# A graph network on one core: features normalised in place, the convolutions' buffers in two pools, and the check of the edge order moved into the second convolution

## The chip, the cores and the metric

The kernel runs on one core of a Trainium2 chip. A core has TensorE (PE; its weight loads are shown apart as PEld), VectorE (DVE), ScalarE (ACT), GpSimd (POOL) and SyncE (SP, which here only issues transfers). Each engine works off its own instructions strictly in the order in which the program lists them. The metric is the device time of one execution in microseconds (us); less is better. A run's time is compared as a median over several executions.

## The reference: what is computed

There are 12,500 nodes with 64 features each and 200,000 edges (`src`, `dst`), the list being sorted by `dst`, and 64 features for each edge. In short:

```python
h = relu(layernorm(x))
h1 = relu(mean_over_edges_into(dst, h[src]) @ W1l.T + b1 + h @ W1r.T)
x = x + mean_over_edges_into(dst, h1[src]) @ W2l.T + b2 + h1 @ W2r.T
h = relu(layernorm(x))
hidden = relu(concat(h[src], h[dst], edge_attr) @ W1 + b1)
x = x + mean_over_edges_of(src, hidden @ W2 + b2)
```

All is float32. The kernel keeps each float32 table as three bfloat16 parts that add up to it.

## The kernel before, in words

**Tiling.** Nodes go in 49 blocks of 256. The edges into one block lie in one window of 128 × 34 entries of the sorted list; where a window begins is worked out on the chip. Inside a window the edges are sorted by the block of their `src`, into 49 cells of at most 128 slots. So there are 49 × 49 = 2401 cells, and each cell joins one source block with one destination block.

**A cell in a convolution.** The numbers of a cell's source nodes are a row in DRAM (`srow_b`). SP loads the rows of 16 cells, broadcast to all partitions, as one tile `srow` of 512 KB (L725). DVE compares it with the partition's node number, which gives the one-hot `turned` (L735). PE multiplies it with the three-part table (`ta` in the first convolution, `tb` in the second) into `got` (L889), ACT casts that to `rows` (L893), DVE makes the one-hot of the destinations, `hot` (L744), and PE adds the rows up in `acc` (L769). After the 49 cells of a destination block `conv` closes it (L806 to L843): ACT copies the sums (L816), DVE forms the mean (L820 to L828), PE transposes and multiplies with the weights (L834, L839), and DVE adds the bias (L841). The first convolution writes its result as three parts into `tb`, the second goes on to the layer norm of the last stage.

**The start.** Four pieces of work are woven into each other by hand: every piece is a generator, and a `yield` is a place where the other pieces get their turn.

* `find_blocks` (L19 to L109) loads the whole `dst` list as 125 × 1600 integers (`find_d`), checks that it does not go down (L31 to L42: each entry against the next; the entry at a row's end by a small tile `find_n` that two more transfers fill), shifts the numbers down to block numbers (L47, L50), counts with small matmuls where each block begins, and leaves `begin_i` (L98) and `bad` (L103). At its end the flags of the order check are transposed by PE (L105) and join `bad` (L108, L109).
* `features` (L470 to L497) normalises x, which lies in the memory of `tb`, in seven parts: a layer norm (L322 to L340), then the split into three parts (L342 to L352) with subtractions on POOL. The normalised values go from `ln_sq` through a Relu into a tile `h1`, the rests into `three_r`. These tiles are in a pool `in` with three buffers.
* `sorter` (L509 to L688) sorts the edges of one block after the other in 13 steps on DVE and PE, and writes the rows (`rows_o`) to DRAM by SP's queue (L660 to L662).
* `clearing` (L270 to L287) fills tables in DRAM with zeros, from a part of `tb` that POOL has set to zero (L700), in transfers of 640 KB and 160 KB on SP's queue.

POOL's `seen` (L699) waits for the last load of x before POOL sets that part to zero, and the integer ramps of `find_blocks` (L53, L57) are behind it on POOL.

**The order around the convolutions.** The convolutions run over groups of 4 cells. The transfers of `srow` are issued two parts of 16 cells ahead. While the first convolution runs, the sorter and the clearing go on; in both, `edge_terms` (POOL's indirect transfers, L385) runs beside. At the end of the first convolution a copy of `bad` goes to `which` (L958), which after the last stage selects between this path's result and a general one.

**Pools and memory.** A tile's memory is given out by its pool. The pool `in` takes the top end of what is free, the pool `layers` (`srow`, `turned`, `hot`, `rows`, then the tiles of `conv`) the other end; `layers` is opened after `in` is closed and partly lies on the same memory. An instruction that writes such memory first waits for the last instruction that used it. Transfers that SP and ACT issue take eight completion semaphores in turn, so each waits for the transfer eight before it.

Of the kernel before, what the change touches and what calls it, by code (L numbers as in the profile page):

```python
# [15 lines left out]
P = 128  # L16


def find_blocks(tc, work, psum, begin_i, bad, dst, nb, blk, win):  # L19
# [8 lines left out]
    d = work.tile([R, C], I32, name="find_d")  # L28
    nc.sync.dma_start(d, dst.rearrange("(r c) -> r c", c=C))

    n = work.tile([R, 2], I32, name="find_n")  # L31
    rows = dst.rearrange("(r c) -> r c", c=C)
    nc.vector.memset(n, 0)
    nc.sync.dma_start(n[0:R - 1, 0:1], rows[0:R - 1, C - 1:C])
    nc.sync.dma_start(n[0:R - 1, 1:2], rows[1:R, 0:1])
    yield
    down = work.tile([R, C], BF, name="find_down")
    nc.vector.tensor_tensor(down[:, 0:C - 1], d[:, 0:C - 1], d[:, 1:C], op=OP.is_gt)
    nc.vector.tensor_tensor(down[:, C - 1:C], n[:, 0:1], n[:, 1:2], op=OP.is_gt)
    yield  # L40
    flags = work.tile([R, 1], FT, name="find_flags")
    nc.vector.tensor_reduce(flags, down, AX.X, OP.max)  # L42


    yield
    q = d
    nc.vector.tensor_scalar(q, d, blk.bit_length() - 1, None, op0=OP.arith_shift_right)  # L47
    yield
    qb = down
    nc.vector.tensor_copy(qb, q)  # L50
    yield
    ids_i = work.tile([R, nb], I32, name="find_ids_i")
    nc.gpsimd.iota(ids_i, pattern=[[1, nb]], base=0, channel_multiplier=0)  # L53
# [6 lines left out]
    first = work.tile([R, 1], FT, name="find_first")  # L60
    nc.vector.tensor_copy(first, q[:, 0:1])
# [13 lines left out]
    for k in range(0, C, F):  # L75
        yield
        pr = psum.tile([nb, F], FT, name="find_pr", bufs=2)
        nc.tensor.matmul(pr, pick, qb[:, k:k + F], start=True, stop=True)
# [22 lines left out]
    nc.vector.tensor_sub(many, line[:, 1:], begin)  # L101
    nc.vector.tensor_scalar(many, many, float(win), None, op0=OP.is_gt)
    nc.vector.tensor_reduce(bad, many, AX.X, OP.max)  # L103
    pf = psum.tile([1, P], FT, name="find_pf")
    nc.tensor.transpose(pf[:, :R], flags, ident[:R, :R])  # L105
    yield
    f = work.tile([1, 1], FT, name="find_f")
    nc.vector.tensor_reduce(f, pf[:, :R], AX.X, OP.max)  # L108
    nc.vector.tensor_max(bad, bad, f)  # L109

@with_exitstack
def fast_path(
# [197 lines left out]
    def bc(ap, n):  # L313
        return ap.unsqueeze(len(ap.shape)).to_broadcast([*ap.shape, n])
# [154 lines left out]

    def features():  # L470
        def some(work, s):
            h = work.tile([P, 2 * CH, D], FT, name="h1", bufs=2)
            xs = xs_all[s].rearrange("p b h d -> p (b h) d")
            yield from layernorm_relu(work, h, xs, 2 * CH, xs)
            yield from three(work, ta[:, s * CH:(s + 1) * CH].rearrange("p b h d -> p (b h) d"), h,
                             nc.gpsimd.tensor_sub)

        def others():
            for _ in range(2):
                if next(finding, found) is found:  # L480
                    found[0] = True
            if sorted_to[0] < STEPS:
                next(sorter)
            next(clearing, None)

        with tc.tile_pool(name="in", bufs=3, side="right") as work:
            line = Line()
            for s in range(NB // CH):
                line.tick(some(work, s))
                others()  # L490
                line.tick()
                others()
# [307 lines left out]
    gather = layers.enter_context(tc.tile_pool(name="gather_ps", bufs=4, space=bass.MemoryType.PSUM))  # L800
    work = layers.enter_context(tc.tile_pool(name="layers", bufs=2))
    next_rows = rows_with_one(work)
    line = Line()
    second = [None]

    def conv(layer, table, w, b, finish, B, acc):  # L806

        if layer:
            xv = second[0].tile([P, 2, D], FT, name="x2", bufs=3)
            if B == FULL:  # L810
                nc.vector.memset(xv[96:P], 0.0)
            a, t = node_rows(x, B, xv)
            nc.sync.dma_start(t, a)
        yield
        v = work.tile([P, 2, W3], FT, name="sums")
        nc.scalar.copy(v, acc[:, :, :W3])  # L816
        yield
        m = work.tile([P, 2, 2, D], FT, name="both")
        t = table[:, B]
        nc.vector.tensor_add(m[:, :, 1], t[:, :, 0:D], t[:, :, D:2 * D])  # L820
        nc.vector.tensor_add(m[:, :, 1], m[:, :, 1], t[:, :, 2 * D:])
        nc.vector.tensor_add(m[:, :, 0], v[:, :, 0:D], v[:, :, D:2 * D])
        nc.vector.tensor_add(m[:, :, 0], m[:, :, 0], v[:, :, 2 * D:D3])
        if layer == 0:
            c = work.tile([P, 2], FT, name="cnt")
# [9 lines left out]
        ct = work.tile([P, 2, P], FT, name="both_t")  # L835
# [4 lines left out]
        o = work.tile([P, 2, D], FT, name="conv")  # L840
        nc.vector.tensor_add(o, acc[:, :, P:P + D], rows(b, 2))  # L841
        yield
        yield from finish(B, o, *((xv,) if layer else ()))  # L843

    def after_conv1(B, o):
        g = work.tile([P, 2, D], FT, name="g", bufs=3)
        nc.scalar.activation(g, o, AF.Relu)
        yield from three(work, tb[:, B], g, nc.vector.tensor_sub)

    def after_conv2(B, o, v):  # L850
        nc.vector.tensor_add(v, v, o)
# [88 lines left out]
    for (layer, c0, c1, part), t, coming in ahead(  # L940
            todo, lambda p: sources(*p[:3]),
            lambda p, r: turned(work, "turned", r, p[2] - p[1])):
        for a, z in part:
            line.tick_behind(some_cells(layer, t, c0, a, z))
            if layer == 0:
                sort_to(z)
                while filled < z:
                    filled += next(clearing, CELLS)
            next(coming, None)
            if layer or a >= 150:  # L950
                beside.passed((z - a) * (1.1, 0.9)[layer])
# [475 lines left out]
```

## Time and profile before

Three runs took 3668.18, 3670.29 and 3679.0 us; the median is 3670.29. The profile shows another execution:

| what | value |
|---|---|
| time of the profiled execution | 3675.2 us |
| its span, first to last instruction | 3673.4 us |
| mean granted TensorE clock | 0.989 of full |
| the start, until the first `turned` | 0 to 90.15 us |
| first convolution | to about 1307 us |
| copy of `bad` to `which` (L958) | 1307.49 us |
| load of `find_d` (781 KB) issued | 0.76 us |

How it is read: a line of the timeline gives the start in us, the length in us, the engine, the program's line, the operation, the tile written and the tiles read with partitions × elements and type, and `xN` where several lie together. In brackets stand the idle time of the engine ahead of it and what ended that. "SPq" is an issue of a transfer on SP's queue, not the transfer itself. "issue" as releaser means that the profile shows nothing that was waited for. A row of windows gives for each stretch its length, then the busy time and the number of instructions of PE, PEld, DVE, ACT and POOL, the granted clock, the mean busy share of the 16 DMA engines, and GB/s.

### The profile page before, as it was taken

To read this page: it belongs to the slowest core of one execution; us is meant where nothing else is said; L and a number is where in the kernel's file an instruction comes from. 1 tells how busy PE (TensorE), PEld (TensorE's weight loads), DVE (VectorE), ACT (ScalarE), POOL (GpSimd) and SP (SyncE) were. 2 spreads that over 40 slices of the span, in tenths; PEclk is the share of its full clock that TensorE was granted. 3 is DMA by queue.
4 is the path that set the end of the run, shared out by engine and by line. 5 is a ranking of instruction groups with operands and counts; after the bars stand their busy time and mean duration, and the time that the engine had idled before them with its cause. 6 is when DMAs were issued, how large, how long until landed. Compare 5 with 4: busy or idle time off the path is not lost.

```text
span 3673.4 us, 126991 instructions
## 1 busy us (share of the span) xinstructions
PE 3419.6 (93%) x50925; PEld 3363.3 (92%) x50925; DVE 3253.3 (89%) x5709; ACT 2506.4 (68%) x5944; POOL 2756.2 (75%) x2335
## 2 busy tenths in 40 slices
PE   1799999899899999999999998999999999999897
PEld 0798999898889999999999998999999999999887
DVE  7999999999899868778787787899989998998998
ACT  3455656565566667777777776788888888887665
POOL 4067787888777877777777773788888888887665
PEclk9999999999999999999999999999999999999999
DMA  6755545555454334444444444766666676666664
GB/s 212 269 163 152 169 155 162 156 167 160 142 164 143 122 120 146 129 141 140 137 137 137 141 129 142 225 215 200 220 208 216 202 219 210 210 201 206 191 219 145
DMA packets 413671, 635.66 MB, mean 173 GB/s; under 512 B 94131, under 2 KB 296247, under 8 KB 413070
## 3 DMA queue, kind: packets, MB, share of 16 engines
q1 hardware_dynamic: 353106, 572.87, 49.9%
q0 software_dynamic: 53312, 51.36, 4.1%
q8 instruction: 399, 6.54, 0.7%
q10 hardware_dynamic: 6652, 3.24, 0.4%
q14 instruction: 202, 1.65, 0.1%
HBM read 474.72 MB, written 155.83 MB: 172 GB/s over the span
## 4 chain that ended last, share of the span: by engine, by line
PE 64%; DVE 24%; DMA 5%; issue 3%; POOL 2%; SPq 1%; ACT 1%; ACTq 0%; DVEq 0%; POOLq 0%
PE acc L769 23%; PE got L889 13%; PE got L1071 12%; PE got L1072 6%; DVE hot L744 6%; DVE turned L735 4%; PE pE L417 3%; DVE hot_r L629 3%; PE pE L402 2%; POOL terms L385 2%; DMA terms_in<-terms 1%; DVE ranks L617 1%; DMA terms<-tb 1%; PE got L1068 1%; PE acc L839 1%
## 5 line engine op out<-in xcount | busy, mean ns | idle before, releaser
L385 POOL DMA_INDIRECT terms<-terms_o,turn_i x1666 | 1929.8, 1158 | 625.9 <-issue 425.1
L893 ACT CAST rows<-got 128x384 bf16<-128x384 f32 x2402 | 1038.3, 485 | 666.0 <-PE got L889 655.2
L769 PEld LDWEIGHTS <-hot 128*128 128x128 bf16 x12006 | 1032.2, 99 | 14.4 <-issue 4.8
L769 PE MATMUL acc<-rows,hot 128*128 128x193 bf16 x9604 | 1010.6, 247 | 0.0
L1083 POOL TENSOR_TENSOR hidden<-hidden 128x512 f32<-128x512 f32 (+1 forms) x602 | 758.5, 1260 | 227.7 <-ACT hidden L1080 144.0
L889 PEld LDWEIGHTS <-turned 128*128 128x128 bf16 x9604 | 813.3, 98 | 89.6 <-DVE turned L735 60.4
L744 DVE TENSOR_TENSOR hot<-dcol,local 128x1024 bf16<-128x1024 bf16 x1202 | 807.9, 683 | 12.7 <-PE acc L769 11.6
L735 DVE TENSOR_SCALAR turned<-srow,nid 128x2048 bf16<-128x2048 bf16 (+1 forms) x906 | 779.4, 874 | 22.7 <-issue 10.8
L1071 PE MATMUL got<-ta,turned 128*128 128x128 bf16 x3920 | 599.1, 220 | 7.3 <-DVE turned L735 7.3
L1071 PE MATMUL got<-tb,turned_d 128*128 128x128 bf16 x3920 | 599.8, 220 | 1.1 <-DVE turned_d L735 1.1
L889 PE MATMUL got<-ta,turned 128*128 128x192 bf16 x4802 | 508.4, 248 | 73.3 <-DVE turned L735 49.4
L1072 PE MATMUL got<-tb,turned_d 128*128 128x64 bf16 x3920 | 546.0, 193 | 0.0
L1072 PE MATMUL got<-ta,turned 128*128 128x64 bf16 x3920 | 545.9, 193 | 0.0
L1095 ACT ACTIVATE hot_a<-every,scol 128x256 bf16<-128x256 bf16 x1196 | 505.4, 493 | 0.0
L889 PE MATMUL got<-tb,turned 128*128 128x192 bf16 x4802 | 494.1, 246 | 0.9 <-DVE turned L735 0.5
L1080 ACT ACTIVATE hidden<-y 128x512 f32<-128x512 f32 (+1 forms) x301 | 190.4, 633 | 270.4 <-DVE y L1077 154.8
L1071 PEld LDWEIGHTS <-turned 128*128 128x128 bf16 x3920 | 362.4, 98 | 8.2 <-issue 7.8
L1071 PEld LDWEIGHTS <-turned_d 128*128 128x128 bf16 x3920 | 359.7, 98 | 1.7 <-DVE turned_d L735 1.7
L1072 PEld LDWEIGHTS <-turned 128*128 128x128 bf16 x3920 | 359.2, 98 | 1.2
L1072 PEld LDWEIGHTS <-turned_d 128*128 128x128 bf16 x3920 | 359.6, 98 | 0.0
L1098 ACT ACTIVATE hot_a<-hot_a 128x1024 bf16<-128x1024 bf16 x299 | 316.2, 1057 | 9.5
L735 DVE TENSOR_SCALAR turned_d<-drow,nid 128x2048 bf16<-128x2048 bf16 (+2 forms) x302 | 316.8, 1091 | 0.0
(220 smaller groups left out, 4912.2 us busy)
## 6 DMA issues: line engine op xcount, KB each, us to landing
srow<-srow_b SPq DMA_DIRECT2D x300, 512.0 KB
srow<-srow_k SPq DMA_DIRECT2D x149, 512.0 KB
drow<-drow_k SPq DMA_DIRECT2D x149, 512.0 KB
terms_in<-terms SPq DMA_DIRECT2D x294, 160.0 KB
edges<-in_edge_attr_dram SPq DMA_DIRECT2D x200, 192.0 KB
terms<-tb SPq DMA_DIRECT2D x200, 160.0 KB
terms<-tb SPq DMA_DIRECT2D x48, 640.0 KB
terms<-terms_o,turn_i POOLq DMA_INDIRECT x1666
```

What stands on the lines that cost most here:

```text
L385: nc.gpsimd.indirect_dma_start(out=terms[j][:], out_offset=bass.IndirectOffsetOnAxis(ap=at[:, c, h:h + 1], axis=0), in_=o[:, c, h], in_off ...
L735: nc.vector.tensor_scalar(o[:, h, :n * S], r[:, :n * S], nid[:, h:h + 1], None, op0=OP.is_equal)
L744: nc.vector.tensor_tensor(o[:, :n], cols.rearrange("p (g c) -> p g c", c=2).unsqueeze(2).to_broadcast([P, n, 2 * P, 2]), local.rearrange(" ...
L769: nc.tensor.matmul(self.acc[B][:, h, :W3], lt, r[:, c, 0:W3], start=k + h == 0, stop=k == row - 1 and h == 1, skip_group_check=True)
L889: nc.tensor.matmul(p[:, (i - c) * D3:(i - c + 1) * D3], t[:, h, (a - c0 + i) * S:(a - c0 + i + 1) * S], table[:, (a + i) % NB, h], start=h ...
L893: nc.scalar.copy(g[:, c:c + m, :D3], p[:, :m * D3].rearrange("p (c d) -> p c d", c=m))
L1071: nc.tensor.matmul(p[:, c], lt, rt[:, 0:2 * D], start=i == 0, stop=False, skip_group_check=True)
L1072: nc.tensor.matmul(p[:, c, 0:D], lt, rt[:, 2 * D:], start=False, stop=i == 3, skip_group_check=True)
L1080: nc.scalar.activation(w[:, :n, 0:D], y[:, :n], AF.Relu)
L1083: nc.gpsimd.tensor_sub(w[:, :n, (i + 1) * D:(i + 2) * D], w[:, :n, j], upper(w)[:, :n, j])
L1095: nc.scalar.activation(q[:, c - k], every, AF.Abs, scale=-1.0, bias=scol[:, scol_at[last] + a + c:scol_at[last] + a + c + 1])
L1098: nc.scalar.activation(q[:, :n - k], q[:, :n - k], AF.Relu, bias=1.0, scale=-2.0)
```

## The change

1. `find_blocks` no longer checks the order. `find_n`, its two transfers, `find_down`, `find_flags`, the transpose and the last two DVE instructions are gone, and with them two yields. The shift and its cast come first; the cast goes to an own tile `find_q`, and `find_first` is copied right behind it.
2. `features` works in place: the normalised values and the rests stay in the memory of `tb`, `h1` and `three_r` are gone, and the pool `in` has two buffers for three. Numbers and kinds of the instructions stay.
3. The tiles of `conv` and `after_conv1` (`sums`, `both`, `cnt`, `both_t`, `conv`, `g`, `three_r`) leave the pool `layers` for a pool `closing`, opened after it. In memory `in` now begins above the part of `layers` that holds `srow`, `turned`, `hot` and `rows`.
4. `order_check` is new. It is opened at the end of the first convolution and goes one step on with every group of the second: it loads the whole `dst` list again, with a 1601st column that holds the first entry of the next row, compares in two halves, takes maxima in halves and quarters, reduces, lets PE transpose, and joins the result with `bad`. Only then is `bad` copied to `which`.

As a consequence, the program's order moves a little elsewhere: DVE's L554 and L555 of the next blocks' sorting come ahead of the first `turned`.

```diff
@@ find_blocks
-    n = work.tile([R, 2], I32, name="find_n")
-    rows = dst.rearrange("(r c) -> r c", c=C)
-    nc.vector.memset(n, 0)
-    nc.sync.dma_start(n[0:R - 1, 0:1], rows[0:R - 1, C - 1:C])
-    nc.sync.dma_start(n[0:R - 1, 1:2], rows[1:R, 0:1])
     yield
-    down = work.tile([R, C], BF, name="find_down")
-    nc.vector.tensor_tensor(down[:, 0:C - 1], d[:, 0:C - 1], d[:, 1:C], op=OP.is_gt)
-    nc.vector.tensor_tensor(down[:, C - 1:C], n[:, 0:1], n[:, 1:2], op=OP.is_gt)
+    nc.vector.tensor_scalar(d, d, blk.bit_length() - 1, None, op0=OP.arith_shift_right)
     yield
-    flags = work.tile([R, 1], FT, name="find_flags")
-    nc.vector.tensor_reduce(flags, down, AX.X, OP.max)
-    yield
-    q = d
-    nc.vector.tensor_scalar(q, d, blk.bit_length() - 1, None, op0=OP.arith_shift_right)
-    yield
-    qb = down
-    nc.vector.tensor_copy(qb, q)
+    q = work.tile([R, C], BF, name="find_q")
+    nc.vector.tensor_copy(q, d)
+    first = work.tile([R, 1], FT, name="find_first")
+    nc.vector.tensor_copy(first, d[:, 0:1])
     yield
...
-    pf = psum.tile([1, P], FT, name="find_pf")
-    nc.tensor.transpose(pf[:, :R], flags, ident[:R, :R])
+
+
+def order_check(tc, work, psum, ident, bad, dst):
...
+    rows = dst.rearrange("(r c) -> r c", c=C)
+    d = work.tile([R, C + 1], I32, name="order_d")
+    nc.vector.memset(d[96:R, C:], 2 ** 30)
+    nc.sync.dma_start(d[:, 0:C], rows)
+    nc.sync.dma_start(d[0:R - 1, C:], rows[1:R, 0:1])
+    for _ in range(4):
+        yield
+    down = work.tile([R, C], BF, name="order_down")
+    nc.vector.tensor_tensor(down[:, 0:C // 2], d[:, 0:C // 2], d[:, 1:C // 2 + 1], op=OP.is_gt)
     yield
-    f = work.tile([1, 1], FT, name="find_f")
-    nc.vector.tensor_reduce(f, pf[:, :R], AX.X, OP.max)
+    nc.vector.tensor_tensor(down[:, C // 2:], d[:, C // 2:C], d[:, C // 2 + 1:], op=OP.is_gt)
+    yield
+    for k in (C // 2, C // 4):
+        nc.vector.tensor_max(down[:, 0:k], down[:, 0:k], down[:, k:2 * k])
+    yield
+    flags = work.tile([R, 1], FT, name="order_flags")
+    nc.vector.tensor_reduce(flags, down[:, 0:C // 4], AX.X, OP.max)
+    yield
+    p = psum.tile([P, 512], FT, name="pX")
+    nc.tensor.transpose(p[0:1, :R], flags, ident[:R, :R])
+    yield
+    f = work.tile([1, 1], FT, name="order_f")
+    nc.vector.tensor_reduce(f, p[0:1, :R], AX.X, OP.max)
     nc.vector.tensor_max(bad, bad, f)
@@ features
-            h = work.tile([P, 2 * CH, D], FT, name="h1", bufs=2)
-            xs = xs_all[s].rearrange("p b h d -> p (b h) d")
-            yield from layernorm_relu(work, h, xs, 2 * CH, xs)
-            yield from three(work, ta[:, s * CH:(s + 1) * CH].rearrange("p b h d -> p (b h) d"), h,
-                             nc.gpsimd.tensor_sub)
+            n = 2 * CH
+            v = xs_all[s].rearrange("p b h d -> p (b h) d")
+            o = ta[:, s * CH:(s + 1) * CH].rearrange("p b h d -> p (b h) d")
...
+            nc.vector.reciprocal(st[:, 1], st[:, 2])
+            nc.vector.tensor_mul(v, v, bc(st[:, 1], D))
+            yield
+            nc.scalar.activation(v, v, AF.Relu)
+            nc.scalar.copy(o[:, :, 0:D], v)
+            yield
+            nc.gpsimd.tensor_sub(v, v, o[:, :, 0:D])
+            yield
+            nc.scalar.copy(o[:, :, D:2 * D], v)
+            yield
+            nc.gpsimd.tensor_sub(o[:, :, 2 * D:], v, o[:, :, D:2 * D])
...
-        with tc.tile_pool(name="in", bufs=3, side="right") as work:
+        with tc.tile_pool(name="in", bufs=2, side="right") as work:
@@ the convolutions
+    closing_work = layers.enter_context(tc.tile_pool(name="closing", bufs=2))
...
-        v = work.tile([P, 2, W3], FT, name="sums")
+        v = closing_work.tile([P, 2, W3], FT, name="sums")
...
             if layer:
+                if ordered is not None and next(ordered, ordered) is ordered:
+                    ordered = None
+                    ordering.close()
+                    nc.vector.tensor_copy(which, bad)
...
-            nc.vector.tensor_copy(which, bad)
             sorting.close()
+            ordering = ExitStack()
+            ordered = order_check(tc, ordering.enter_context(tc.tile_pool(name="order", bufs=1, side="right")),
+                                  psum_x, ident, bad, dst)
```

More of the change, by code (lines that the diff above doesn't have):

```diff
@@ L59, in find_blocks @@
     nc.vector.tensor_copy(own, own_i)
-    first = work.tile([R, 1], FT, name="find_first")
-    nc.vector.tensor_copy(first, q[:, 0:1])
     less = work.tile([R, nb], FT, name="find_less")
@@ L77, in find_blocks @@
         pr = psum.tile([nb, F], FT, name="find_pr", bufs=2)
-        nc.tensor.matmul(pr, pick, qb[:, k:k + F], start=True, stop=True)
+        nc.tensor.matmul(pr, pick, q[:, k:k + F], start=True, stop=True)
         nc.vector.tensor_scalar(row[:, k:k + F], pr, own[:nb], None, op0=OP.is_lt)
@@ L103, in find_blocks @@
     nc.vector.tensor_reduce(bad, many, AX.X, OP.max)
-    pf = psum.tile([1, P], FT, name="find_pf")
-    nc.tensor.transpose(pf[:, :R], flags, ident[:R, :R])
-    yield
-    f = work.tile([1, 1], FT, name="find_f")
-    nc.vector.tensor_reduce(f, pf[:, :R], AX.X, OP.max)
+def order_check(tc, work, psum, ident, bad, dst):
+    nc = tc.nc
+    R = 125
+    C = dst.shape[0] // R
+    rows = dst.rearrange("(r c) -> r c", c=C)
[7 more added lines that the diff above has]
+    nc.vector.tensor_tensor(down[:, 0:C // 2], d[:, 0:C // 2], d[:, 1:C // 2 + 1], op=OP.is_gt)
+    yield
+    nc.vector.tensor_tensor(down[:, C // 2:], d[:, C // 2:C], d[:, C // 2 + 1:], op=OP.is_gt)
[11 more added lines that the diff above has]
+    nc.vector.tensor_reduce(f, p[0:1, :R], AX.X, OP.max)
     nc.vector.tensor_max(bad, bad, f)
@@ L471, in some @@
         def some(work, s):
-            h = work.tile([P, 2 * CH, D], FT, name="h1", bufs=2)
-            xs = xs_all[s].rearrange("p b h d -> p (b h) d")
-            yield from layernorm_relu(work, h, xs, 2 * CH, xs)
-            yield from three(work, ta[:, s * CH:(s + 1) * CH].rearrange("p b h d -> p (b h) d"), h,
-                             nc.gpsimd.tensor_sub)
+            n = 2 * CH
+            v = xs_all[s].rearrange("p b h d -> p (b h) d")
+            o = ta[:, s * CH:(s + 1) * CH].rearrange("p b h d -> p (b h) d")
+            st = work.tile([P, 3, n], FT, name="ln_st", bufs=3)
+            nc.vector.tensor_reduce(st[:, 0], v, AX.X, OP.add)
+            nc.vector.scalar_tensor_tensor(v, bc(st[:, 0], D), -1.0 / D, v, op0=OP.mult, op1=OP.add)
+            yield
+            sq = work.tile([P, n, D], FT, name="ln_sq")
+            nc.scalar.activation(sq, v, AF.Square)
+            yield
+            nc.vector.tensor_reduce(st[:, 1], sq, AX.X, OP.add)
+            yield
+            nc.scalar.activation(st[:, 2], st[:, 1], AF.Sqrt, bias=small, scale=1.0 / D)
+            yield
+            nc.vector.reciprocal(st[:, 1], st[:, 2])
+            nc.vector.tensor_mul(v, v, bc(st[:, 1], D))
+            yield
+            nc.scalar.activation(v, v, AF.Relu)
+            nc.scalar.copy(o[:, :, 0:D], v)
+            yield
+            nc.gpsimd.tensor_sub(v, v, o[:, :, 0:D])
+            yield
+            nc.scalar.copy(o[:, :, D:2 * D], v)
+            yield
+            nc.gpsimd.tensor_sub(o[:, :, 2 * D:], v, o[:, :, D:2 * D])
         def others():
@@ L814, in conv @@
         yield
-        v = work.tile([P, 2, W3], FT, name="sums")
+        v = closing_work.tile([P, 2, W3], FT, name="sums")
         nc.scalar.copy(v, acc[:, :, :W3])
         yield
-        m = work.tile([P, 2, 2, D], FT, name="both")
+        m = closing_work.tile([P, 2, 2, D], FT, name="both")
         t = table[:, B]
@@ L824, in conv @@
         if layer == 0:
-            c = work.tile([P, 2], FT, name="cnt")
+            c = closing_work.tile([P, 2], FT, name="cnt")
             nc.vector.tensor_scalar(c, v[:, :, D3], 1.0, None, op0=OP.max)
@@ L834, in conv @@
             nc.tensor.transpose(acc[:, h, :P], m[:, h].rearrange("p a d -> p (a d)"), ident)
-        ct = work.tile([P, 2, P], FT, name="both_t")
+        ct = closing_work.tile([P, 2, P], FT, name="both_t")
         nc.scalar.copy(ct, acc[:, :, :P])
@@ L839, in conv @@
             nc.tensor.matmul(acc[:, h, P:P + D], ct[:, h], w, start=True, stop=True)
-        o = work.tile([P, 2, D], FT, name="conv")
+        o = closing_work.tile([P, 2, D], FT, name="conv")
         nc.vector.tensor_add(o, acc[:, :, P:P + D], rows(b, 2))
@@ L845, in after_conv1 @@
     def after_conv1(B, o):
-        g = work.tile([P, 2, D], FT, name="g", bufs=3)
+        g = closing_work.tile([P, 2, D], FT, name="g", bufs=3)
         nc.scalar.activation(g, o, AF.Relu)
-        yield from three(work, tb[:, B], g, nc.vector.tensor_sub)
+        yield from three(closing_work, tb[:, B], g, nc.vector.tensor_sub)
     def after_conv2(B, o, v):
```

## The prediction

> **What bounds the kernel now.** I read the page first: busy shares and the chain that ended last, for the kernel's limit.
>
> ```profile
> span 3673.4 us, 126991 instructions
> ...
> PE 3419.6 (93%) x50925; PEld 3363.3 (92%) x50925; DVE 3253.3 (89%) x5709; ACT 2506.4 (68%) x5944; POOL 2756.2 (75%) x2335
> ...
> PE 64%; DVE 24%; DMA 5%; issue 3%; POOL 2%; SPq 1%; ACT 1%; ACTq 0%; DVEq 0%; POOLq 0%
> ```
>
> TensorE and VectorE (DVE) share the kernel. The change touches two short places: the start (0 to 93 us) and the passage into the second convolution (from 1307 us). Whatever it does to the rest, it does by shifting it. So next I read both places, by time, engine by engine. First DVE near the end of the start:
>
> ```profile
> 76.67 2.38 DVE L338 TENSOR_TENSOR ln_sq<-tb,ln_st 128x896 f32<-128x896 f32 x1
> 78.98 0.34 DVE L708 COPY wcat<-pW 128x64 f32<-128x64 f32 x2
> 90.15 1.42 DVE L735 TENSOR_SCALAR turned<-srow,nid 128x2048 bf16<-128x2048 bf16 x2 [10.83 <-issue]
> ```
>
> DVE has nothing to do for 10.8 us, until the first rows (`srow`) have landed. Who holds them is on POOL and on SP's queue:
>
> ```profile
> 84.01 1.88 POOL L352 TENSOR_TENSOR ta<-three_r,ta 128x896 bf16<-128x896 f32 x1 [1.05 <-ACT ta L350]
> 85.95 0.25 POOL L781 MEMSET rows<- 128x8 bf16 x5
> ```
>
> ```profile
> 67.18 0.34 SPq L660 DMA_DIRECT2D srow_b<-rows_o  x1
> ...
> 68.23 9.99 SPq L279 DMA_DIRECT2D terms<-tb  x9
> 85.91 6.00 SPq L725 DMA_DIRECT2D srow<-srow_b  x3
> ```
>
> The load is issued within 0.1 us of the end of POOL's last subtraction, 85.9: it waits for that tile's memory. But ahead of it in the same queue stand nine clearing transfers of 640 KB each. The windows of stages show whether these are done (stretch; length; busy time of PE, PEld, DVE, ACT, POOL, each with its instructions; granted clock; DMA share; GB/s):
>
> ```profile
> 78.00:84.00 6.00, 0.00 (x0) 0.00 (x0) 1.32 (x3) 3.77 (x4) 3.87 (x3) 1.00 1.03 391
> 84.00:86.00 2.00, 0.00 (x0) 0.00 (x0) 0.00 (x0) 0.00 (x0) 1.93 (x3) 1.00 0.18 67
> 86.00:88.00 2.00, 0.00 (x0) 0.00 (x0) 0.00 (x0) 0.00 (x0) 0.19 (x5) 1.00 0.31 127
> 88.00:90.00 2.00, 0.00 (x0) 0.00 (x0) 0.00 (x0) 0.00 (x0) 0.00 (x0) 1.00 0.79 322
> ```
>
> At 391 GB/s the DMA engines are full until 84; 67 GB/s over the next 2 us is 0.3 us more of that rate. So they are truly idle only from 84.3 to about 87.3, where the rows' data starts (127 GB/s over 86 to 88). That is 3.0 us, not 10.8.
>
> **Part 1: the pools are split.** The first `srow`, `turned` and POOL's memset of `rows` no longer lie on features' buffers, so SP may issue the load behind the ninth clearing transfer. Then it starts when the DMA engines come free: −3.0 us. Bounds: −2 (the load has its own 1.4 us from issue to data at 85.9 to 87.3, of which some could remain), −4 (the clearing's tail shared with the rows). The clearing itself, 9 × 640 KB = 5.9 MB, at 391 GB/s 15 us, is unchanged and stays ahead.
>
> **Part 2: the order check leaves the start.** DVE is without a gap from about 15 to 70 us, and the row writer that ends in L660 is behind it. Removed from it are L38 1.82, L39 0.15, L42 1.82, L108 0.27, L109 0.15 = 4.2 us. But what comes next is not free:
>
> ```profile
> 15.45 1.82 DVE L38 TENSOR_TENSOR find_down<-find_d 125x1599 bf16<-125x1599 int32 x1
> ...
> 17.38 1.82 DVE L42 TENSOR_REDUCE find_flags<-find_down 125x1 f32<-125x1600 bf16 x1
> ...
> 25.81 0.28 DVE L55 CAST find_ids<-find_ids_i 125x49 f32<-125x49 int32 x1
> ```
>
> ```profile
> 23.60 0.18 POOL L699 COPY seen<-tb 1x1 f32<-1x1 f32 x1 [19.15 <-DMA tb<-in_x_dram]
> 23.72 1.37 POOL L700 MEMSET tb<- 128x1536 bf16 x1
> 25.04 0.17 POOL L53 IOTA find_ids_i<- 125x49 int32 x1
> ```
>
> L55 needs POOL's iota, and POOL stands behind `seen`, which waits for the last load of x. In the changed order L55 comes two turns earlier: straight behind the shift (0.98), its cast (0.99), `find_first` (0.14) and `hot` (1.02), so DVE is there at 15.4 + 3.1 = 18.5. The iota ends at 25.2; with the loads of x waiting for an earlier transfer (they queue on ACT behind eight shared completion semaphores, and two are gone) I put it up to 0.9 earlier, 24.3. So DVE stands 5.8 us, and steps which filled that time, L601 0.45, L602 0.43, L333 1.08, L325 1.07, L328 1.09, less overlaps 3.8, come behind it. Before, all this is done when L65 ends, 26.6. After: 24.3, L55 to L65 0.8, the moved steps 3.8: 28.9, or 2.3 later. L108 and L109 no longer come after that: the row writer is +1.9. Bounds: −0.4 (the iota 2.3 earlier still, at 22.0, so that only L108 and L109 are won), +3.5 (the iota not earlier, +0.9, and one collision with POOL more, +0.7: `hot_r` took 2.91 us beside POOL's subtraction and 1.34 without, half of that). Since L660 and the nine transfers wait for that writer, all of it comes through to the rows.
>
> **Part 3: features in place.** Same instructions, same shapes, on ACT, POOL and DVE; `h1` and `three_r` are gone, and the wait of a rewritten tile is for an operation of its own chain. The pool has two buffers for three. POOL and ACT stand idle between these steps (8.2, 4.7 and 4.6 us ahead of L348), which covers it: 0. If that cover were gone, one subtraction, 1.9 us.
>
> **Part 4: ids ahead of the first `turned`.** L554 and L555, 0.37 and 0.27 us, at 92.1 after the first `turned`, come into the idle time before it: −0.6.
>
> **Part 5: the check in the second convolution.** DVE gets two compares of 800 (0.91 each, half of L38), maxima of 800 and 400 (0.53 and 0.30, scaled from L744's 0.68 for 1024), a reduction of 400 (0.46, a quarter of L42), two tiny ones and the copy to `which`: 3.6 us. There PE is the bound:
>
> ```profile
> 1300.00:1320.00 20.00, 16.30 (x183) 15.42 (x182) 12.82 (x30) 11.50 (x31) 15.55 (x15) 1.00 0.33 104
> 1320.00:1340.00 20.00, 20.00 (x233) 19.94 (x231) 15.54 (x30) 13.53 (x35) 15.42 (x16) 1.00 0.49 149
> ```
>
> DVE has 7.2 and 4.5 us free in these; the one-hots are made ahead (`hot` has five buffers), so 3.6 us, at most 1.8 between two yields, stay beside PE. If that cover were gone: 3.6. PE's transpose of the flags is on the path: 0.37, say +0.3. The load of the whole list is new there. At the start 800 KB took from its issue at 0.76 to SP's next freed slot at 11.89, 11.1 us; issued at about 1308.7, it lands about 1319.8, while DVE arrives at the first compare, four groups behind the issue and in the changed order behind the `hot` of 1318.71, at about 1319. What queues behind the compare on DVE are `turned` and `hot`; PE has some 3 us of these in hand (five buffers of `hot`, a group of four cells each 1.4 us, less those in use). On SP, the clearing is over and `srow` stands behind it in the queue, two parts ahead. I take +1 (bounds 0, and +5 with a landing 8 us late less the 3 in hand). SP's read of `which` moves behind the check, and ahead of an `srow` load that waits for a still later `turned`: 0.
>
> As a rule against this: the Trainium skill, "DMA: Bandwidth & Descriptors", section "Why a DMA increments its semaphore by 16 and not by 1", says a transfer uses the largest number of engines up to 16 that divides its outer dimension, so 125 rows give five. An estimate from it: 160 KB on each of five, at this case's 391/16 = 24.4 GB/s, is 6.6 us, 5 less than the row says, and the term would be 0 for +1, were it alone on them.
>
> **Sum.** −3.0 + 1.9 + 0 − 0.6 + 0.3 + 1 = −0.4 us. The profiled execution took 3675.2 (span 3673.4 and 1.8 around it), 4.9 above the median of the runs, 3670.3: that is its own excess, not the change's. The median less 0.4: 3670.
>
> **The rivals.** A, the sum as it stands: 3667 to 3673.
> B, the start's gain stays whole: DVE does not stand at L55 because the loads of x end earlier than I think, so part 2 is −0.4 to −4.2 in place of +1.9. Then −2.7 to −6.5: 3664 to 3668; with all 10.8 us of DVE's idle time gone 3659. For it: first convolution is DVE's (181 to 196 us of each 200 busy), so what DVE wins counts. Against it: `seen` at 23.6.
> C, slower: DVE stands at the first compare in the second convolution, since the load lands late among `srow` and `terms` transfers. It decides from a landing later than 1319 + 3 = 1322, 13.3 us after issue; each us more costs one. 18 to 21 us after issue give +5 to +8: 3675 to 3678. For it: 11.1 us at the start with less beside it at first. Against it: only 104 to 149 GB/s are moved there.
> D, the rows come no earlier: the writer slips by 3.1 + 0.6 or more, as its upper bound of +3.5 nearly does: then +2 to +3.5: 3673.
>
> **How the numbers follow.** A 0.48, B 0.26, C 0.16, D 0.10. Forecast A, 3670. Of B about two fifths ends under 3664, of C a third above 3677; 3658 to 3680 leaves out less than 2 in 10 and holds the bounds of parts 2 and 5. A measurement of this kernel tells 0.3% (11 us) from no change: faster than 3659 is B with all idle time and more, 0.12; slower than 3681 is C with the landing still later, 0.08; within, 0.80.
>
> **What would show it.** Part 1: the first `srow` issue right behind the ninth clearing transfer, its POOL wait gone, and DMA with no gap at 84 to 87. Part 2: DVE idle some 5 us before `find_ids`, released by POOL; L660's issue at 69 in place of 67.2. Part 4: `ids_f` before the first `turned`. Part 5: `order_down` with no idle time in front of it, or one of 1 us, and PE full from 1320 to 1340. Wrong it would be if DVE's first `turned` starts before 86 or after 91, or if the second convolution's first groups show PE waiting for `turned`.

## The result

Twenty executions of each kernel, taken together: the changed kernel 3684.01 us (median; 3674.79 to 3699.81), the kernel before 3674.22 us (3668.18 to 3687.56; the three runs shown above are among these, two of them the fastest of all). The ratio is 1.0023, with a 95% interval of 1.0014 to 1.0032. So it is slower, by 5 to 12 us, 8.4 at the ratio and 9.8 between the medians, which is inside the 0.3% that the prediction called no change, and outside its range of 3658 to 3680. The profiled execution took 3688.91 us (span 3687.1), 4.9 above its median. In the experiments up to e16 the kernel before itself took 4516 to 4528 us (medians; see the last section), and beside e17 and e18 3674.74; so each ratio there is against the kernel before that ran beside it.

The page of the changed kernel:

```profile
span 3687.1 us, 127002 instructions
...
PE 3427.0 (93%) x50925; PEld 3370.2 (91%) x50925; DVE 3269.5 (89%) x5711; ACT 2505.4 (68%) x5944; POOL 2777.7 (75%) x2335
...
PE 63%; DVE 21%; issue 5%; DMA 5%; POOL 4%; SPq 1%; ACT 1%; POOLq 0%; DVEq 0%; ACTq 0%
```

Shares of 3.7 ms show nothing of 8 us. What does is the start of the same instruction in two profiles: the n-th `hot` (L744 before, L772 after) is there 1202 times in both. "Later" is the start in the profile after less that in the profile before:

| `hot` | in the kernel | before, us | later by, us |
|---|---|---|---|
| 1st | first group | 91.5 | 1.4 |
| 301st | middle of the first convolution | 708.1 | 1.8 |
| 591st | end of the first convolution | 1285.7 | 10.8 |
| 641st | 40 groups into the second | 1370.3 | 15.1 |
| 1201st | end of the second | 2272.5 | 15.1 |

At the end of the span it is 13.7; the medians are 9.8 apart, so some 4 us of that belong to these two executions. There are three places: the start (1.4), the second half of the first convolution (9.0, of which 7.5 fall between the 301st and the 401st), and the entry of the second (4.3). Timeline of DVE in the start, changed kernel:

```profile
24.29 0.26 DVE L42 CAST find_ids<-find_ids_i 125x49 f32<-125x49 int32 x1 [5.84 <-POOL find_ids_i L40]
...
49.83 2.02 DVE L645 TENSOR_TENSOR ranks<-ranks 128x340 bf16<-128x340 bf16 x1
...
54.08 2.52 DVE L495 TENSOR_TENSOR tb<-tb,ln_st 128x896 f32<-128x896 f32 x1
...
91.59 1.42 DVE L763 TENSOR_SCALAR turned<-srow,nid 128x2048 bf16<-128x2048 bf16 x2 [8.09 <-DMA srow<-srow_b]
```

and SP's queue:

```profile
70.51 0.33 SPq L688 DMA_DIRECT2D srow_b<-rows_o  x1
...
71.55 9.95 SPq L287 DMA_DIRECT2D terms<-tb  x9
81.67 11.69 SPq L753 DMA_DIRECT2D srow<-srow_b  x3
```

and the windows at the place where the DMA engines had been idle before:

```profile
84.00:86.00 2.00, 0.00 (x0) 0.00 (x0) 0.00 (x0) 1.16 (x2) 1.95 (x2) 1.00 1.04 397
86.00:88.00 2.00, 0.00 (x0) 0.00 (x0) 0.00 (x0) 0.83 (x1) 1.14 (x1) 1.00 1.01 294
```

DVE stands 5.84 us for POOL's ramp, as worked out; the load of the first rows is issued right behind the ninth clearing transfer, its wait for POOL is gone, and the DMA engines have no gap from 84 to 88. But the row writer comes at 70.51, 3.3 later and not 1.9, so the rows come 1.4 later instead of earlier.

At the entry of the second convolution, waits in the changed kernel from 1318 to 1342 us (engine, instruction and releaser; us in total, times, longest):

```profile
ACT terms_o L433 <- DMA terms<-terms_o,turn_i: 3.9, 1, 3.9
PEld pE L410 <- ACT terms_o L433: 3.9, 1, 3.9
PE pE L410 <- ACT terms_o L433: 3.6, 1, 3.6
```

Before, PE's wait at this transpose was 1.53 us:

```profile
1315.71 0.65 PE L402 MATMUL pE<-ident,edges 128*128 128x128 f32 x4 [1.53 <-ACT terms_o L425]
```

ACT cannot overwrite `terms_o` until POOL's scatter (its indirect transfer of the edge terms) out of it has landed; PE's transpose needs what ACT writes, and the matmuls of the cells stand behind the transpose. Behind the longer wait PE is also slower for a while, PE after and then the windows of 1330 to 1340, after and before:

```profile
1329.04 0.88 PE L410 MATMUL pE<-ident,edges 128*128 128x128 f32 x4 [3.64 <-ACT terms_o L433]
1329.71 1.49 PE L918 MATMUL got<-tb,turned 128*128 128x192 bf16 x8
```

```profile
1330.00:1340.00 10.00, 10.00 (x101) 9.80 (x100) 8.99 (x18) 5.38 (x14) 7.90 (x7) 0.86 0.49 156
1330.00:1340.00 10.00, 10.00 (x119) 9.98 (x117) 8.65 (x17) 6.84 (x17) 7.71 (x8) 1.00 0.26 86
```

Eight matmuls into `got` take 1.49 us there and 0.82 elsewhere, at a granted clock of 0.86 over these 10 us. An estimate from PE's rows: 2.1 us of longer wait and 1.5 of slower matmuls make 3.6 of the 4.3.

The same chain does the damage between 500 and 1000 us. There, before:

```profile
ACT terms_o L425 <- DMA terms<-terms_o,turn_i: 6.7, 3, 3.2
```

and after:

```profile
ACT terms_o L433 <- DMA terms<-terms_o,turn_i: 42.1, 19, 4.3
```

Why the scatters are late can be read from the same two traces. In the first convolution POOL issues them late: the first scatter starts 1.0 us later than before, the 201st (513 us) 4.4 and the 301st (660 us) 11.4, while `hot` is still under 2 us late there. Of the 10.4 us in between, 9.7 are the scatters' own time on POOL (372.6 us for 300 of them, 362.9 before); from issue to landing they take as long as before (medians of 3.2 to 3.5 us in both). At the entry it is the landing: the six scatters issued from 1319.3 to 1327.7 take 5.1 to 6.8 us to land, and beside them runs the list's load, issued at 1320.2; the eight ahead of them take 2.1 to 3.7, and those at this place before 2.2 to 4.4. ACT had waited 2.9 us for a scatter twice ahead of the list already (at 1301.7 and 1313.7), so the list is not the whole of it.

### The profile page after: what moved, and what is told of

Its sections match the earlier page's. It is cut to its first block, busy times and chain, and to the rows that moved or that the text cites. A ratio compares the mean times of both kernels' runs of the same rounds, so it can differ in the third digit from the quotient of the medians.

```text
span 3687.1 us, 127002 instructions
## 1 busy us (share of the span) xinstructions
PE 3427.0 (93%) x50925; PEld 3370.2 (91%) x50925; DVE 3269.5 (89%) x5711; ACT 2505.4 (68%) x5944; POOL 2777.7 (75%) x2335
## 4 chain that ended last, share of the span: by engine, by line
PE 63%; DVE 21%; issue 5%; DMA 5%; POOL 4%; SPq 1%; ACT 1%; POOLq 0%; DVEq 0%; ACTq 0%
PE acc L797 22%; PE got L918 13%; PE got L1106 12%; PE got L1107 6%; DVE hot L772 5%; DVE turned L763 4%; PE pE L425 3%; POOL terms L393 3%; DVE hot_r L657 2%; PE got L1103 2%; PE pE L410 2%; DMA terms<-tb 1%; DVE ranks L645 1%; DMA terms<-terms_o,turn_i 1%; PE acc L868 1%
## 5 line engine op out<-in xcount | busy, mean ns | idle before, releaser
L393 POOL DMA_INDIRECT terms<-terms_o,turn_i x1666 | 1949.3, 1170 | 624.6 <-issue 434.0
L772 DVE TENSOR_TENSOR hot<-dcol,local 128x1024 bf16<-128x1024 bf16 x1202 | 807.9, 683 | 13.2 <-PE acc L797 12.1
```

What stands on the lines that cost most here:

```text
L393: nc.gpsimd.indirect_dma_start(out=terms[j][:], out_offset=bass.IndirectOffsetOnAxis(ap=at[:, c, h:h + 1], axis=0), in_=o[:, c, h], in_off ...
L772: nc.vector.tensor_tensor(o[:, :n], cols.rearrange("p (g c) -> p g c", c=2).unsqueeze(2).to_broadcast([P, n, 2 * P, 2]), local.rearrange(" ...
```

## The experiments

Two theories stood after the profile. **T**: beside the start, the load of the edge list at the entry of the second convolution costs, by making scatters land late. **R**: it costs nothing; the scatters fall behind in the first convolution. Where whole times could not tell them apart (below), places inside the profiles are compared.

**No check at all; the load split; the ramps first; the check put back.** Four kernels, each one edit of the changed kernel:

```diff
 # e1: bad goes to which at the end of the first convolution
-                if ordered is not None and next(ordered, ordered) is ordered:
...
+            nc.vector.tensor_copy(which, bad)
 # e2
-    nc.sync.dma_start(d[:, 0:C], rows)
+    nc.sync.dma_start(d[0:112, 0:C], rows[0:112])
+    nc.sync.dma_start(d[112:R, 0:C], rows[112:R])
 # e3: in find_blocks, behind the load of find_d
+    nc.gpsimd.iota(ids_i, pattern=[[1, nb]], base=0, channel_multiplier=0)
...
+    nc.gpsimd.iota(own_i, pattern=[[0, 1]], base=0, channel_multiplier=1)
     yield
 # e4: find_blocks as before, which as in e1
```

> The order of the edges is not checked at all here: order_check is left out, and bad goes to which at the end of the first convolution, as before. Theory T: the load of the whole list at the entry of the second convolution makes the scatters of edge_terms land late, ACT's terms_o stands behind them and PE behind ACT; that is 3.8 us and, with the clock's pause after it, up to 5.5. Then this run is 3.5 to 5.5 us shorter than the changed kernel, ratio to before 1.0008 to 1.0014, and ACT's wait of 3.9 us at the entry is gone. Rival R: the list's load costs nothing, the time is lost in the first convolution, where POOL's scatters fall behind. Then the ratio stays at 1.0020 to 1.0026.

> The list is loaded in the second convolution in two transfers, of 112 and of 13 rows, in place of one of 125. Theory T with few engines: 125 rows are carried by few of the sixteen DMA engines, and what queues on these is late. Then the load lands within 6 us, ACT's wait at the entry of the second convolution is under 2 us, and the time is 2 to 4 us under the changed kernel: ratio 1.0012 to 1.0018. Rival: it is the 800 KB that count, not how they are spread: wait and time as in the changed kernel, 1.0020 to 1.0026.

> find_blocks gives its two ramps to POOL at the very start, ahead of seen. Theory T: DVE's 5.8 us of standing at find_ids go, the row writer comes 3 to 5 us earlier (its first transfer at 65 to 67 in place of 70.5), the first turned at 87 to 88.5 in place of 91.6; the time is 3 to 4.5 us under the changed kernel, ratio 1.0010 to 1.0016. Rival: the clearing transfers fill the DMA engines in any case, the first turned stays after 90 and the ratio at 1.0020 to 1.0026.

> The order check is back in find_blocks as before; features in place and the divided pool stay. Theory T: only the wait of the first srow load for POOL goes, the row writer stays at 67; the first turned at 87 to 88.5 in place of 90.15, and nothing is lost later: 2 to 3 us under before, ratio 0.9990 to 0.9996. Rival R: working in place, or the moved tiles, make POOL's scatters fall behind in the first convolution: ratio 1.0010 to 1.0020 although the start is shorter.

Against 4522.87 us before, the ratios were 1.0002 [0.9975, 1.0029], 0.9984 [0.9950, 1.0017], 0.9978 [0.9944, 1.0012] and 0.9985 [0.9954, 1.0016]: no answer on T and R. The start answers:

| kernel | row writer, us | first `turned`, us |
|---|---|---|
| before | 67.18 | 90.15 |
| changed | 70.51 | 91.59 |
| e1, no check | 70.55 | 92.17 |
| e2, split load | 70.23 | 91.34 |
| e3, ramps first | 65.45 | 86.99 |
| e4, check back | 66.99 | 88.04 |

Profiles of one program order agree here within 1.2 us: the first `turned` lies from 89.8 to 90.2 in three of the order before, and from 91.0 to 92.2 in eleven of the changed one. e4 has the pool's part without the check's: the writer where it was, the first rows 2.1 us earlier (1.9 in e8, the same kernel again). e3 takes DVE's wait away and gets back 5.1 us at the writer and 4.6 at the rows. With the ramps first, DVE goes on without a pause (timeline of e3):

```profile
17.56 1.02 DVE L621 TENSOR_TENSOR hot<-keys,kexp 128x1666 bf16<-128x1666 bf16 x1
18.49 0.18 DVE L43 CAST find_ids<-find_ids_i 125x49 f32<-125x49 int32 x1
```

**The changed kernel, e1 and e4 again, and the first rows ahead of the clearing.** The new one, e5, is e3 with two more moves:

```diff
             if sorted_to[0] < STEPS:
                 next(sorter)
-            next(clearing, None)
+                next(clearing, None)
+            else:
+                held[0] += 1
...
             line.tick_behind(some_cells(layer, t, c0, a, z))
+            while held[0]:
+                held[0] -= 1
+                next(clearing)
...
-            nc.gpsimd.memset(r[:, :, D3:], 1.0)
+            nc.vector.memset(r[:, :, D3:], 1.0)
```

> The changed kernel again, beside the others of this call, for a second profile. Both theories: ratio 1.0014 to 1.0032. Theory T (the list's load at the entry of the second convolution): ACT's wait for scatters at the entry is 3 us or more again. Rival R (POOL's scatters fall behind in the first convolution): ACT waits for them there some 40 us in sum again, against 15 in the kernel before.

> Without the order check, as in the first trial of it. T: 3.5 to 5.5 us under the changed kernel in this call. R: as the changed kernel, within 2 us.

> The check back in find_blocks, features in place and divided pool kept, as in the first trial. T: 2 to 3 us under before, ratio 0.9990 to 0.9996. R: ratio 1.0010 to 1.0020.

> The changed kernel with three moves in the start: the ramps of find_blocks first on POOL, the nine clearing transfers behind the first three loads of srow, and DVE in place of POOL setting the ones in rows. If the first rows are held by the clearing ahead of them, the first turned comes at 78 to 80, when DVE is done with features, 10 us before the kernel before, and since DVE bounds the first convolution 7 to 12 us of it stay up to its end; the time is then that much under the changed kernel plus 1.4, ratio to before 0.998 to 1.0005. Rival: the clearing put later delays rows and scatters in the first 100 us of the convolution, and less than 4 us stay.

Against 4521.47 us: the changed kernel 0.9976 [0.9944, 1.0007], no check 0.9998 [0.9976, 1.0020], check back 0.9996 [0.9972, 1.0020], none told from before. ACT's waits for scatters, which T expected at the entry and R in the first convolution, are not in these profiles (ACT is idle ahead of `terms_o` for under 1 us in all, against 59 in the changed kernel's profile above), so neither chain was at work and both expectations failed for these runs. e5 had 0.9947 [0.9916, 0.9978], 0.5% under before; its first `turned` started at 78.28, right behind DVE's last step of the start. Its SP queue:

```profile
65.23 0.33 SPq L690 DMA_DIRECT2D srow_b<-rows_o  x1
...
66.84 16.34 SPq L755 DMA_DIRECT2D srow<-srow_b  x3
83.22 9.53 SPq L286 DMA_DIRECT2D terms<-tb  x8
```

**A third try of the pair.**

> Without the order check, for a third time: in the first two calls TensorE stood still for about 0.8 ms of the convolutions in the kernel before as well, which hid differences of a few us. Where it doesn't: theory T (the list's load at the entry of the second convolution costs) 3.5 to 5.5 us under the changed kernel, ratio 1.0008 to 1.0014; rival R (POOL's scatters fall behind in the first convolution) within 2 us of the changed kernel. The first turned is at 91 to 92 in either.

> The changed kernel beside it: ratio 1.0014 to 1.0032. T: ACT's wait for scatters at the entry of the second convolution is 3 us or more. R: ACT's waits for scatters in the first convolution sum to some 40 us, against 15 in the kernel before.

Against 4516.49 us: 1.0015 [0.9982, 1.0047] and 1.0003 [0.9971, 1.0034]. Inconclusive again.

**Half the gathers left out**, to rid PE of its standing still:

```diff
-                for h in range(2):
-                    nc.tensor.matmul(..., start=h == 0, stop=h == 1, skip_group_check=True)
+                nc.tensor.matmul(..., start=True, stop=True, skip_group_check=True)
```

> The kernel before with half of the gathers left out: of each pair of matmuls into got only the one for the even nodes is made, in both convolutions (so the sums lack the odd nodes). It is the base for the next run. PE has a quarter less to do in the convolutions; if that ends its standing still there, DVE and POOL set the pace as in the profile of the kernel before, and the convolutions take some 1.2 and 0.8 ms or less: differences of a few us can be told then.

> The changed kernel with the same half of the gathers left out. Against the run before it: both theories have +1.4 us at the first turned. T (the list's load at the entry of the second convolution): +3 to +5 more between the last hot of the first convolution and the twentieth of the second. R (POOL's scatters fall behind in the first convolution): +5 to +10 between the first hot and the last of the first convolution, and ACT waits for scatters there two times as long as in the base.

4284.01 and 4278.23 us, against 4528.38 for the whole kernel before: the standing still stayed (PE was busy for 75 to 77 of each 100 us looked at in e11's convolutions), and the pair told nothing.

**No scatters.** This ended it. The indirect transfer of `scatter` is taken out of the kernel before (e13), of the changed kernel (e14), of e1 (e15) and of e5 (e16):

```diff
-                    nc.gpsimd.indirect_dma_start(
-                        out=terms[j][:], out_offset=bass.IndirectOffsetOnAxis(ap=at[:, c, h:h + 1], axis=0),
...
```

> The kernel before without POOL's indirect scatters: the edge terms are computed but never written to their tables, which stay zero. It is the base of this call. If PE's standing still in the convolutions comes with the scatters, it is gone here, and the convolutions are as long as in the first profile (1.2 and 0.95 ms) or shorter; otherwise the time stays near 4500 us.

> The changed kernel without the scatters. If the loss behind the start goes through late scatters (theories T, at the entry of the second convolution, and R, over the first), only the start's part is left: +1 to +2 us against the base. If the list's load holds up srow loads or DVE instead (rival C of the prediction), +3 to +6 us are left, and they lie at the entry of the second convolution.

> As the run before, and without order_check. If the list's load costs nothing without scatters: the same as the run before, +1 to +2 us against the base. If C holds: 2 to 5 us under the run before.

> The changed kernel with the three moves in the start (ramps first, clearing behind the first loads of srow, DVE sets the ones), without the scatters. If DVE's lead of some 11 to 13 us at the first turned stays to the end of the first convolution: 8 to 13 us under the changed kernel without scatters. If the clearing put later takes it back: under 4 us.

Medians of six executions: 3655.52, 3660.77, 3659.50 and 3652.09 us, beside 4520.70 for the kernel before with its scatters. Differences of the means, with 95% intervals from redrawing the six times of each: e14 less e13 +3.0 [−1.4, +6.7], e15 less e14 +0.1 [−3.0, +3.6], e16 less e14 −9.0 [−12.5, −5.2]. Whole times thus don't show the check's cost (e15 less e14). By the start of the n-th `hot` against e13, one profile each, it is much sharper (e17 and e18, described below, ran later than e13 to e16):

| `hot` | e14 changed | e15 no check | e16 rows first | e17 split load | e18 later compare, rows first |
|---|---|---|---|---|---|
| 1st | +1.3 | +2.0 | −8.9 | +1.4 | −8.7 |
| 591st | −0.2 | +0.4 | −6.9 | −1.9 | −8.1 |
| 641st | +2.7 | +0.4 | −3.9 | −1.8 | −8.0 |
| 1201st | +2.9 | +0.7 | −3.7 | −1.6 | −7.8 |
| end of span | +6.8 | +5.9 | −3.3 | +3.1 | −9.2 |

(From the 1201st on, all run the same code. What is added there, −1.4 to +5.2 us, comes behind 3334 us, in the last part of the last stage; until there the differences stay within 0.5 us of those at the 1201st (e16: 1.2). What brings it was not looked for; it is why e14 and e15, 2.2 apart at the 1201st, end 0.9 apart.)

Both kernels with the check lose 2.9 and 3.0 us between the 591st and the 641st; the one without it loses nothing. So the check itself costs 3 us at this place, without any scatter: rival C of the prediction. T, which goes through scatters, had expected nothing here. DVE in e14:

```profile
1301.40 0.75 DVE L759 TENSOR_SCALAR turned<-srow,nid 128x2048 bf16<-128x2048 bf16 x1
1305.05 0.99 DVE L104 TENSOR_TENSOR order_down<-order_d 125x800 bf16<-125x800 int32 x1 [2.90 <-DMA order_d<-in_dst_dram]
```

PE in e14:

```profile
1307.37 0.75 PE L914 MATMUL got<-tb,turned 128*128 128x192 bf16 x7 [0.91 <-DVE turned L759]
...
1310.83 0.27 PE L115 MATMUL pX<-ident,order_flags 125*1 125x125 f32 x1 [1.62 <-DVE order_flags L112]
```

and SP's issue of the load in e14:

```profile
1294.26 0.32 SPq L99 DMA_DIRECT2D order_d<-in_dst_dram  x1
```

DVE reaches the compare 7.9 us after the issue and stands 2.9 us for the list. PE then waits 0.9 us for the next `turned`, and 1.6 us at the transpose of the flags, which stands in PE's order and waits for DVE's reduction, late by as much. 0.9 + 1.6 is the loss, but for 0.4.

**Why the list is late, and whether only the wait costs.** e17 is e14 with the load of e2; e18 is e16 with twelve `yield`s in place of four between load and compare.

> The changed kernel without scatters, the list loaded in 112 and 13 rows. In the changed kernel without scatters the load landed 10.8 us after its issue (five of sixteen parts of its semaphore count came with the data), DVE stood 2.9 us for it, and the second convolution stayed 2.9 us behind. If few engines are the cause: the load lands 7 to 8.5 us after its issue, DVE stands under 0.8 us, the step at the entry is under 1 us. If the 800 KB are: 2.5 to 3 us again.

> Without scatters: the three moves in the start (ramps first, clearing behind the first rows, DVE sets the ones), and the first compare of the check twelve groups behind the load in place of four. If DVE's standing at the compare, and PE's transpose behind it, are all that the check costs, the step at the entry is under 0.8 us, and the lead of the start, 6 to 8 us at the end of the first convolution, is whole at the start of the last stage; the time is 8 to 12 us under the changed kernel without scatters. If the five engines that the load fills cost as such (late srow loads), 1.5 to 3 us are lost there all the same.

Times: 3659.90 us (five executions) and 3650.11 us (six), beside 3674.74 for the kernel before with its scatters. The step at the entry is 0.1 us in both (table above): −1.9 to −1.8 and −8.1 to −8.0. In e17's whole time, against e14's 3660.77, the gain does not show. DVE in e17 finds the list there:

```profile
1299.72 0.75 DVE L760 TENSOR_SCALAR turned<-srow,nid 128x2048 bf16<-128x2048 bf16 x1
1300.46 0.99 DVE L105 TENSOR_TENSOR order_down<-order_d 125x800 bf16<-125x800 int32 x1
```

The times at which the trace has the load's semaphore counted up (e14's 125 rows, issued at 1294.26; e17's 112 rows, issued at 1292.58):

```
e14: once at 1294.72; then 1304.60 1304.61 1304.76 1304.77 1305.02
e17: 16 times from 1297.57 to 1300.01
```

Five counts come with the data of the 125 rows, the last 10.8 us after issue; with 112 rows sixteen do, the last 7.4 us after it. The Trainium skill, "DMA: Bandwidth & Descriptors", section "Why a DMA increments its semaphore by 16 and not by 1", says that only the engines a transfer uses count up with their data, that the rest of the 16 is written at once, and that the number used is the largest up to 16 that divides the slowest dimension. By that rule 125 rows give five and 112 sixteen, and the runs agree (one early update 0.5 us after issue, then five; sixteen). The prediction had weighed this and taken the longer row for its sum. The `srow` load behind the list in e14 has eleven of its counts by 1300.1 and the last five only from 1305.9 to 1306.2; e18, with the same unsplit load, has the same lateness (eleven by 1292.8, five from 1297.8) and loses nothing, so that lateness alone was free.

## Why the prediction was wrong

**Part 1, the pool (−3.0): right in its mechanism, somewhat less; 2.1 measured** (e4: 88.04 against 90.15; 1.9 in e8; bounds −2 to −4). The gap of the DMA engines and the nine clearing transfers ahead of the rows were the right thing to read, and 10.8 us of idle DVE were not to be had by this. e5 shows where the rest lay: with the ramps first and the clearing behind the rows the first `turned` starts 11.9 us earlier than before.

**Part 2, the check out of the start (+1.9): right in its mechanism, mis-sized; 3.3 measured.** DVE stood 5.84 us for the ramp (5.8 expected, at 24.3). The other 1.4 are collisions with POOL's subtractions, which the prediction had as a bound only (+0.7 for one). Between 24 and 70 us DVE now meets POOL in six instructions: `find_begin` 1.64, L645 with 2.02 us (0.32 before), L495 with 2.52 (1.09 before), `hot_r` 2.90, L495 2.62 and `pos_f` 1.87. Before, it was `find_begin` 1.64, `most` 1.17, `hot_r` 2.91, `ln_sq` 2.62, `pos_f` 1.87, and L612 by 0.6. Against the short case of each (`find_begin` 0.19, taken from `find_line`, `most` 0.18, `hot_r` 1.34, `pos_f` 0.19) the sums are 9.3 and 7.8: 1.5 more. Each of them starts while POOL subtracts and ends behind it. For L645 POOL's row is:

```profile
48.82 2.82 POOL L500 TENSOR_TENSOR tb<-tb,ta 128x896 f32<-128x896 f32 x1 [5.45 <-ACT ta L498]
```

All six took the same time within 0.02 us in every one of the eleven profiles with this start, so this was not chance but the new order's phase.

At the first `hot`, parts 1 and 2 make −1.1 in the prediction and +1.4 in the profiles (+1.1 from e11 to e12 and +1.3 from e13 to e14). That is between A and rival D, which had the writer 3.7 late or more. The start is thus 2.5 us of the miss, and the one part of it that all three pairs of profiles show.

**Part 3 (0): not told apart.** e4 includes it and is 2.1 us ahead at the first rows; no run did it alone. **Part 4 (−0.6): moved as forecast, its worth not shown.** `ids_f` now comes at 74.75, ahead of the first `turned`. The lateness of 1.4 at the first `hot` is 0.8 some 80 us later, but between e13 and e14 it grows there from 1.3 to 1.9.

**Part 5, the check in the second convolution (+1.3): this step failed.** In the changed kernel itself the waits it reckoned with were as it said: the list landed 11.3 us after its issue (11.1 expected), and DVE, held through ACT and PE, came only after 11.8 and did not stand. What was lost there, 4.3 us, went through the scatters, for which the term had no price. Without scatters the landing was right again (10.8), but DVE, expected 10 us after the issue, came after 7.9, stood 2.9 and the kernel lost as much. The 3 us of one-hots that PE was to have in hand it had, about: DVE's 2.90 of standing and 0.99 of compare came through to the next `turned` as 0.91. Mis-sized was the transpose of the flags, which the sum had at its own length of 0.3: it is itself an instruction in PE's order, waits for the late DVE, and cost 1.62. The prediction had this as rival C with a chance of 0.16, deciding from a landing 13.3 us after issue; in these runs DVE stands from 7.9 on.

**The first convolution (no term): this step failed too.** "Whatever it does to the rest, it does by shifting it" put it at nothing. In the profile of the changed kernel 9.0 us are lost in it, through POOL's scatters, which fall 10 us behind by 660 us, and ACT's waits for them (42.1 us against 6.7 between 500 and 1000 us). Without scatters it loses nothing (e14 goes from +1.3 to −0.2).

**The sum.** The forecast was −0.4 us; measured are 8.4 (0.23% of 3674), with an interval of 5 to 12. Of the 14 us between 3670 and 3684.01 another 3.9 are no part of the change: the sum began at 3670.29, the median of three executions, where twenty give 3674.22. Without scatters the changed kernel is 2.9 us late at the end of the second convolution, the check's step being all that is left by then (the start's 1.3 is gone at the 591st, and why was not looked into); the whole times allow that (+3.0 [−1.4, +6.7]) and much else. The rest of the 8.4 goes, in the one profile of the changed kernel, through the scatters, and both theories are at work in it: R in the first convolution, T at the entry, as far as scatters landing late beside the list show it. That they fall behind is read from that execution; that it is a lasting property of the changed kernel was not shown. POOL is busy for 77 to 81 of each 100 us from 200 to 800 us in both kernels, with 0.3 us of issue before each scatter, so that a small loss could grow into a queue; that is argued, and no second pair of whole kernels ran without PE's standing still (last section). Why its scatters took longer on POOL stays open.

## What to carry to other kernels

Before an engine is freed of work early in its order, look at what comes next in that order and who feeds it: here 4.2 us of DVE work had helped to hide a wait for POOL (5.8 us with that work gone), and a ramp that depends on nothing stood behind a wait for the last input. A transfer that is moved beside other work needs its landing time set against the moment when an in-order engine reaches the first use, and each further instruction of the moved piece on another engine (here a transpose on PE) is one more place where lateness comes through. And where a queue is in order, look at what stands in it ahead of a load, and not only at the wait that delays its issue: here the nine clearing transfers cost some 9 us (e5 against e3, which differ in one more small move), the pool's wait 2.

## What the runs showed of the hardware that was not expected

* In the same program, PE stood still for about a fifth of the time in the convolutions in e1 to e12: between 500 and 600 us PE was busy for 79 of 100 us (e1, window line below; DVE 68, POOL 53), against 92 in the kernel before at first, and for 17.5 of its 21 idle us the profile shows nothing that was waited for. The matmuls were slower too, 101 ns of busy time each against 82, at a granted clock of 0.84 against 0.98. Without POOL's indirect scatters it did not happen (3655.52 against 4520.70 us side by side), with a quarter of the convolutions' matmuls left out it did (4284.01). Beside e17 and e18 it was absent with scatters too. What brings it on was not found.

```profile
500.00:600.00 100.00, 79.04 (x779) 71.60 (x778) 67.65 (x127) 43.39 (x116) 52.78 (x48) 0.84 0.33 100
```

* A transfer of 125 rows gets five counts with its data (e14), and the 512 KB load behind it, which gets sixteen, has its last five 6 us after the other eleven.
* A short DVE instruction that starts beside a subtraction on POOL can take that subtraction's rest: 2.02 us in place of 0.32 for L645 (128x340), at the same instruction in all eleven profiles of one program order.
